# Moving a turned attention tile across partitions: four wide transfers per round in place of sixteen square ones

## The chip, the cores and the metric

The kernel runs on one core of a Trainium2 chip. The metric is device time in microseconds (us), from the first to the last instruction of one execution with what lies around it. Three executions of the kernel before took 3247.21, 3250.87 and 3253.22 us, so the median is 3250.87 us.

The core has five engines with a queue each: PE (TensorE, matrix products, with its weight loads shown apart as PEld), DVE (VectorE), ACT (ScalarE), POOL (GpSimd) and SP (SyncE, which only issues transfers here). Transfers run on 16 DMA engines that all queues share. In the profile a transfer that SP issues is on queue q1 and one that POOL issues on queue q0.

## The reference, cut to what matters

Four batches of 1024 tokens, 256 wide, go through a block of four residual steps: attention A (16 heads of 64), a feed-forward step, attention B (16 heads of 64 with low-rank projections and a rotary turn of q and k), and the same feed-forward step again. Everything is float32. The two attentions share this core:

```python
scores = jnp.einsum('bhsd,bhtd->bhst', q, k) * scale
attn = jax.nn.softmax(scores, axis=-1)
out = jnp.einsum('bhst,bhtd->bhsd', attn, v)
```

So each attention has 4 x 16 score matrices of 1024 queries by 1024 keys. The feed-forward steps are `gelu(x @ w1 + b1) @ w2 + b2` with 1024 hidden values, and the change does not touch them.

## The kernel before, in words

**Tiling.** Heads go in pairs: 4 batches x 8 pairs = 32 groups per attention. A group has 8 steps of 128 queries, so an attention has 256 steps. Two steps make a round (`HB = 2`), so there are 128 rounds per attention and 256 in all. `attention` (L190) lays out pieces of work by step, and `steps_with` (L339) emits them in a fixed order; every engine then works through its own queue in that order.

**One step** `s` does the following for 128 queries and the two heads `j` of the pair:

- `scores` (L238, matmul L247): per head a tile `sc` of 128 queries (partitions) by 1024 keys in PSUM. There are three such buffers.
- `exponentials` (L253): DVE takes the row maximum (L258), and ACT writes `exp` into the tile `p` (L260). Before the change a key's place in the row is split as (k, c, i) with 16 k, 2 c and 32 i, and head `j` fills the columns `c` of its own half, in runs of 64 values.
- `invert` (L266): the reciprocal of the row sum (DVE) is spread by ACT over a 17th block of `p` (L269), so that it travels with the probabilities.
- `turn` (L274): DVE transposes 32x32 blocks of `p` into the tile `T` (L280). Afterwards keys lie along partitions, but only within blocks: the 32 partitions of group `a` hold the keys of query block `a`, and the four key groups `c` lie one after another along the free axis.

**The move.** The product with `v` wants all keys of a head on 64 partitions, so `T` (one per round, two buffers) is copied to `pT` (two buffers), square by square: square (a, c) goes from the 32 partitions of group `a` to the 32 partitions of group `c`, 32 rows of 1,088 values (136 KB). There are 16 squares per round. `squares` orders them so that consecutive ones come from groups two apart (0 and 2, or 1 and 3) and go to groups two apart.

- `send` (L298, transfer L304) issues them: SP the first ones directly after the second `turn` of the round, POOL the last five (`POOL_DMA = 5`) in the next step.
- In attention A (`kept=0`) all 16 squares are sent: 11 by SP, 5 by POOL. In attention B (`kept=1`) square (0, 0) stays on its partitions and ACT copies it (`keep`, L296); SP sends 10 and POOL 5.

**After the move.** Two rounds later (`LAG = 5` steps) `weigh` (L306, matmul L313) multiplies with `v`, `take` (L319) copies the sums (ACT) and scales them by the 17th block (POOL, L325), and in the step after that `project` (L327, matmuls at L176) adds the output projection to the residual (ACT L335, POOL L337).

**What sets the order around the change.** SP's queue holds, in this order, a round's squares and then, at some steps, weight loads (in attention B: `wuq`, `wuk`, `wuv` at L849 and `wo` at L221 and L223). SP's first square of round `h` waits for the second turn of the round, and for `weigh` and `take` of round `h-2`, which used the same `pT` buffer. The first turn of round `h+2` waits until the squares of round `h` have been read out of the `T` buffer. Each queue also has eight completion semaphores for its transfers; a transfer waits until the one that used its semaphore before has landed. POOL carries, besides its five squares, the additions to the residual, the scaling at L325 and, in attention B, the rotary products (L870 to L872) and their two transfers (`turned`, L865).

Of the kernel before, what the change touches and what calls it, by code (L numbers as in the profile page):

```python
# [9 lines left out]
F32 = mybir.dt.float32  # L10
AF = mybir.ActivationFunctionType
# [4 lines left out]
P = 128  # L16
# [9 lines left out]
SQ = 32  # L26
# [3 lines left out]
LAG = 5  # L30
NK = 2 * NT + 1
SENT = NG * HB * NK * SQ
POOL_DMA = 5
NK2 = S // DH
EPS = 1e-5
EARLY = 0.5
# [12 lines left out]
def hybrid_block_kernel(  # L49
# [137 lines left out]
                    start=(i == 0), stop=(i == len(parts) - 1),  # L187
                )

    def attention(prep_batch, prep_pair, wo, loader, lead, kept):  # L190

        pairs = [(b, pr) for b in range(B) for pr in range(NF)]
        steps = [(g, qs) for g in range(len(pairs)) for qs in range(NT)]
        n = len(steps)
        pieces, first = {}, []
        tiles, wos = {}, {}

        def load_out(g):

            wos[g] = wop.tile([P, HB, D], F32, tag="wo", name="wo")
            rows = wo[ts(pairs[g][1], P), :]  # L220
            loader.dma_start(wos[g][:, 0], rows)  # L221
            for j in range(2):
                loader.dma_start(wos[g][ts(j, DH), 1], rows[ts(1 - j, DH), :])  # L223

        for g, (b, pr) in enumerate(pairs):
            for k, f in prep_batch(b) if pr == 0 else ():
                first.append(f) if g == 0 else pieces.setdefault(NT * g - 4 * NT + k, []).append(f)
            tiles[g], load, work = prep_pair(b, pr)
            if g < 2:
                first.insert(g, load)  # L230
            else:
                pieces.setdefault(NT * g - NT - lead - EARLY, []).append(load)
            pieces.setdefault(NT * g - 1 - EARLY, []).append(lambda g=g: load_out(g))
            for k, f in work:
                first.append(f) if g == 0 else pieces.setdefault(max(NT * g - NT + k, -1 - EARLY), []).append(f)
        sc, probs, total, T, pT, av, oT = {}, {}, {}, {}, {}, {}, {}

        def scores(s):  # L238
            g, qs = steps[s]
            qT, kT = tiles[g]["qT"], tiles[g]["kT"]  # L240
            for j in range(2):
                sc[s, j] = ps_sc.tile([P, S], F32, tag="sc", name="sc")
            for m in range(S // 512):
                for half in range(2):
                    for j in range(2):
                        rows = slice(j * DH, (j + 1) * DH)
                        nc.tensor.matmul(  # L247
                            sc[s, j][ts(half, DH), ts(m, 512)],
                            qT()[rows, ts(2 * qs + half, DH)], kT()[rows, ts(m, 512)],
                            start=True, stop=True,  # L250
                        )

        def exponentials(s, j):  # L253
            if j == 0:
                probs[s] = pp.tile([P, NK, NG, SQ], F32, tag="p", name="p")
                total[s] = small.tile([P, 2], F32, tag="total", name="total")
            nmax = small.tile([P, 1], F32, tag="nmax", name="nmax")
            nc.vector.tensor_reduce(nmax, sc[s, j], AX.X, ALU.max, negate=True)  # L258
            place = j ^ (s % HB)
            nc.scalar.activation(  # L260
                probs[s][:, :NK2, ts(j, 2), :],
                sc.pop((s, j)).rearrange("p (k c i) -> p k c i", c=2, i=SQ), AF.Exp,
                bias=nmax, accum_out=total[s][:, place : place + 1],
            )

        def invert(s):  # L266
            t = total.pop(s)
            nc.vector.reciprocal(t, t)  # L268
            nc.scalar.copy(  # L269
                probs[s][:, NK2].rearrange("p (j c) i -> p j (c i)", j=2),  # L270
                t.unsqueeze(2).to_broadcast([P, 2, DH]),
            )

        def turn(s):  # L274
            h, q = divmod(s, HB)
            if q == 0:
                T[h] = tp.tile([P, SENT], F32, tag="T", name="T").rearrange(
                    "p (c q k i) -> p c q k i", c=NG, q=HB, k=NK
                )
            nc.vector.transpose(  # L280
                T[h][:, :, q, :, :].rearrange("p c k i -> p k c i"), probs.pop(s)
            )

        squares = [
            ((a + 2 * i) % NG, (c + 2 * (i ^ x)) % NG)
            for x in range(2) for a in range(2) for c in range(2) for i in range(2)
        ]


        sent = [ac for ac in squares if ac not in [(a, a) for a in range(kept)]]

        def keep(h):
            for a in range(kept):
                nc.scalar.copy(pT[h][ts(a, SQ), a], T[h][ts(a, SQ), a])  # L296

        def send(h, engine, which):  # L298
            if h not in pT:
                pT[h] = ptp.tile([P, SENT], F32, tag="pT", name="pT").rearrange(  # L300
                    "p (a q k i) -> p a q k i", a=NG, q=HB, k=NK
                )
            for a, c in which:
                engine.dma_start(pT[h][ts(c, SQ), a], T[h][ts(a, SQ), c])  # L304

        def weigh(h):  # L306

            v = tiles[HB * h // NT]["v"]()
            av[h] = [group(P) for q in range(HB)]
            for k in range(NK2):  # L310
                for q in range(HB):
                    for j in range(2):
                        nc.tensor.matmul(  # L313
                            av[h][q][ts(j ^ q, DH)], v[ts(j, DH), k, :],
                            pT[h][ts(j, DH), :, q, k, :],
                            start=(k == 0), stop=(k == NK2 - 1),
                        )

        def take(h):  # L319

            oT[h] = otp.tile([P, HB, P], F32, tag="oT", name="oT")
            for q, sums in enumerate(av.pop(h)):
                nc.scalar.copy(oT[h][:, q], sums)  # L323
            parts = oT[h].rearrange("p q (a i) -> p a q i", i=SQ)
            nc.gpsimd.tensor_mul(parts, parts, pT.pop(h)[:, :, :, NK2, :])  # L325

        def project(h):  # L327
            g, t0 = divmod(HB * h, NT)
            b, pr = pairs[g]
            po = group(HB, D)  # L330
            for t in range(HB):
                paired(po[:, t, :], [(oT[h][:, t], [wos[g][:, t]] * 2)])
            oT.pop(h)
            got = tmp.tile([P, HB, D], F32, tag="tmp", name="got")
            nc.scalar.copy(got, po)  # L335
            xd = xs[b][:, t0 : t0 + HB, :]
            nc.gpsimd.tensor_add(xd, xd, got)  # L337

        def steps_with(others):  # L339
            for k, f in others:  # L340
                pieces.setdefault(k, []).append(f)
            for s in range(-1, n + LAG + 1):
                h, part = divmod(s - LAG, HB)
                ahead = 0 <= s + 1 < n
                if 0 <= s < n:
                    invert(s)
                if ahead:
                    scores(s + 1)
                if part == 1 and 0 <= s // HB - 1 < n // HB:
                    send(s // HB - 1, nc.gpsimd, sent[len(sent) - POOL_DMA :])  # L350
                if part == 1 and 0 <= h < n // HB:
                    project(h)
                if ahead:
                    exponentials(s + 1, 0)
                for f in pieces.get(s - EARLY, ()):
                    f()
                if part == 0 and 0 <= h < n // HB:
                    weigh(h)
                if ahead:
                    exponentials(s + 1, 1)  # L360
                if part == 0 and 0 <= h < n // HB:
                    take(h)
                if 0 <= s < n:
                    turn(s)
                if part == 0 and 0 <= s // HB - 1 < n // HB:
                    keep(s // HB - 1)
                    T.pop(s // HB - 1)
                if part == 0 and 0 <= s < n:
                    send(s // HB, nc.sync, sent[: len(sent) - POOL_DMA])
                for f in pieces.get(s, ()):  # L370
                    f()

        return first, steps_with
# [331 lines left out]
    def layer_a():  # L705
# [69 lines left out]

        later = [(4 + i, lambda i=i: rows.measure(2 + i // TQ, i % TQ)) for i in range(6 * TQ)]
        later += [(4 + 6 * TQ, lambda: rows.finish[2]())]
        first, steps = attention(batch_a, pair_a, wo_a, nc.gpsimd, lead=3, kept=0)
        loads, xn, pair = first[:2], first[2:14], first[14:]

        def measured(qb):
# [15 lines left out]
    def layer_b(rows):  # L797
# [92 lines left out]
            work += [(4 + 2 * qb - EARLY, lambda qb=qb: values(qb)) for qb in range(NQB)]  # L890
            return {name: lambda name=name: made[name] for name in ("qT", "kT", "v")}, load, work

        return attention(batch_b, pair_b, wo_b, nc.sync, lead=5, kept=1)


    n_steps = B * NF * NT
# [72 lines left out]
```

## Time and profile before

The profiled execution took 3250.15 us, and its span in the profile is 3248.4 us.

| | before |
|---|---|
| median of three executions | 3250.87 us |
| profiled execution | 3250.15 us |
| span, mean granted clock | 3248.4 us, 0.996 |
| PE busy | 3164.4 us, 97% |
| DVE busy | 2723.5 us, 84% |
| ACT busy | 2137.9 us, 66% |
| POOL busy | 2002.1 us, 62% |
| exponential L260, mean of one | 1119 ns, 1024 of them |
| maximum L258, mean of one | 1218 ns, 1024 of them |
| turn L280, mean of one | 2436 ns, 512 of them |
| square issued by SP / by POOL | 2688 / 1280, 136 KB each, 4.7 us median to landing |
| copied square L296, mean of one | 1096 ns, 128 of them |
| chain that ended last | PE 69%, SP's queue 12%, DMA 6%, DVE 5%, ACT 4% |

Busy time of an engine says how long it had work in hand, not that it set the pace. The question in each stage is which wait ends last there. For the DMA engines the profile gives packets, bytes and the time that packets took as a share of 16 engines' time. A row of a square is one packet of 4,352 bytes, so the time of a row is that share times 16 times the length of the window, divided by the rows in it.

### The profile page before, as it was taken

What the parts mean: (1) busy time and instruction counts of PE and PEld (TensorE: products, weight loads), DVE (VectorE), ACT (ScalarE), POOL (GpSimd) and SP (SyncE); (2) the same over time, 40 slices, a digit from 0 to 9 for tenths busy, and PEclk for the clock granted to TensorE, in tenths of its full rate; (3) what the DMA queues carried; (4) which work ended last, traced back from release to release, by engine and by line L of the source; (5) the groups of instructions that cost most, each with busy time, mean ns of one, the idle gap of its engine ahead of it and who ended that gap; (6) DMA issues with size and microseconds to landing.
All of it is one profiled execution on the core that took longest, in us unless ns stands there. A gap on an engine that the chain in (4) does not pass through costs nothing.

```text
span 3248.4 us, 128967 instructions
## 1 busy us (share of the span) xinstructions
PE 3164.4 (97%) x53648; PEld 2092.2 (64%) x53648; DVE 2723.5 (84%) x2686; ACT 2137.9 (66%) x4400; POOL 2002.1 (62%) x2782
## 2 busy tenths in 40 slices
PE   8999999999999999999999999999999999999999
PEld 4666666666666666668866566666666666655688
DVE  7988888888888888966569989998999999999554
ACT  5666666666666666655447777777778777777542
POOL 4544545455444545442249889899899889886311
PEclk9999999999999999999999999999999999999999
DMA  8888888888888888850029889988989899988200
GB/s 228 217 224 215 224 224 228 217 219 222 221 217 225 219 231 223 221 150 1 4 74 244 225 228 243 242 237 236 246 243 243 234 240 246 238 235 221 57 20 27
DMA packets 244709, 642.29 MB, mean 198 GB/s; under 512 B 74304, under 2 KB 102976, under 8 KB 244128
## 3 DMA queue, kind: packets, MB, share of 16 engines
q1 hardware_dynamic: 161104, 397.60, 48.0%
q0 software_dynamic: 83024, 236.44, 26.0%
q8 instruction: 426, 6.98, 1.0%
q14 instruction: 155, 1.27, 0.1%
HBM read 43.39 MB, written 4.19 MB: 15 GB/s over the span
## 4 chain that ended last, share of the span: by engine, by line
PE 69%; SPq 12%; DMA 6%; DVE 5%; ACT 4%; issue 3%; POOL 1%; DVEq 0%; ACTq 0%; POOLq 0%
PE sc L247 20%; PE mm L313 19%; PE mm L176 15%; SPq L304 11%; DMA pT<-T 5%; PE pw L495 4%; PE mm L185 4%; PE mm L495 3%; PE mm L615 2%; DVE T L280 2%; DVE nmax L258 1%; ACT p L260 1%; PE ph L604 1%; ACT gT L529 1%; PE mm L162 1%
## 5 line engine op out<-in xcount | busy, mean ns | idle before, releaser
L258 DVE TENSOR_REDUCE nmax<-sc 128x1 f32<-128x1024 f32 x1024 | 1204.5, 1218 | 214.3 <-PE sc L247 211.3
L260 ACT ACTIVATE p<-sc,nmax 128x1024 f32<-128x1024 f32 x1024 | 1145.3, 1119 | 322.3 <-DVE nmax L258 322.2
L280 DVE STREAM_TRANSPOSE T<-p 128x2176 f32<-128x2176 f32 x512 | 1247.3, 2436 | 48.4 <-DMA pT<-T 18.4
L247 PE MATMUL sc<-kT,qT 64*64 64x512 f32 x8192 | 1082.5, 598 | 11.9 <-ACT p L260 10.3
L313 PEld LDWEIGHTS mm<-pT,v 64*64 64x64 f32 x32768 | 949.5, 133 | 140.7 <-issue 98.5
L313 PE MATMUL mm<-pT,v 64*64 64x128 f32 x32768 | 983.0, 269 | 9.6 <-issue 8.5
L304 POOL DMA_DIRECT2D pT<-T x1280 | 629.6, 499 | 125.5 <-PE sc L247 57.7
L325 POOL TENSOR_TENSOR oT<-oT,pT 128x256 f32<-128x256 f32 x256 | 187.0, 730 | 696.3 <-ACT oT L323 623.0
L247 PEld LDWEIGHTS sc<-kT,qT 64*64 64x64 f32 x8192 | 332.8, 133 | 401.6 <-issue 274.5
L337 POOL TENSOR_TENSOR x<-x,got 128x512 f32<-128x512 f32 x256 | 331.0, 1293 | 25.8 <-ACT got L335 22.0
L335 ACT COPY got<-mm 128x512 f32<-128x512 f32 x256 | 150.0, 586 | 281.8 <-PE mm L176 281.8
L176 PE MATMUL mm<-wo,oT 128*64 128x256 f32 x2048 | 279.9, 394 | 24.1 <-POOL oT L325 22.8
L176 PEld LDWEIGHTS mm<-wo,oT 128*64 128x64 f32 x2048 | 124.9, 136 | 273.2 <-POOL oT L325 226.5
L269 ACT COPY p<-total 128x128 f32<-128x128 f32 x512 | 151.9, 297 | 198.6 <-DVE total L268 192.4
L176 PE MATMUL mm<-hT,w 128*64 128x512 f32 x1024 | 243.4, 597 | 0.9 <-ACT hT L165 0.9
L260 ACT ACTIVATION_READ_ACCUMULATOR p<-sc,nmax 128x1 f32 x1024 | 205.2, 200 | 0.0
L185 PEld LDWEIGHTS mm<-w,hT 128*64 128x64 f32 x4096 | 140.9, 138 | 71.3 <-issue 69.4
L871 POOL TENSOR_TENSOR turned<-turned,sin_sb 128x512 f32<-128x512 f32 x128 | 163.8, 1279 | 0.0
L409 POOL TENSOR_TENSOR x<-x,b_sb 128x256 f32<-128x256 f32 x64 | 48.8, 777 | 170.6 <-ACT xn L156 170.6
L296 ACT COPY pT<-T 32x1088 f32<-32x1088 f32 x128 | 140.3, 1096 | 4.9 <-DMA pT<-T 1.1
L185 PE MATMUL mm<-w,hT 128*64 128x64 f32 x4096 | 140.9, 222 | 0.2 <-ACT kT L758 0.2
L176 PEld LDWEIGHTS mm<-hT,w 128*64 128x64 f32 x1024 | 73.3, 138 | 96.8 <-issue 75.0
(145 smaller groups left out, 2928.5 us busy)
## 6 DMA issues: line engine op xcount, KB each, us to landing
pT<-T SPq DMA_DIRECT2D x2688, 136.0 KB, 4.7
pT<-T POOLq DMA_DIRECT2D x1280, 136.0 KB, 4.7
turned<-kT POOLq DMA_DIRECT2D x128, 128.0 KB, 3.4
turned<-qT POOLq DMA_DIRECT2D x128, 128.0 KB, 3.5
w<-in_wqkv_a POOLq DMA_DIRECT2D x96, 128.0 KB, 6.0
wo<-in_wo_a POOLq DMA_DIRECT2D x32, 128.0 KB, 5.4
wo<-in_wo_a POOLq DMA_DIRECT2D x64, 64.0 KB, 5.5
wo<-in_wo_b SPq DMA_DIRECT2D x32, 128.0 KB, 4.0
```

What stands on the lines that cost most here:

```text
L176: nc.tensor.matmul(out[ts(j, DH)], lhsT[:, ts(j, DH)], rhs[j], start=(first and i == 0), stop=(last and i == len(parts) - 1),)
L185: nc.tensor.matmul(out[ts(j, DH)], lhsT, rhs[:, ts(j, DH)], start=(i == 0), stop=(i == len(parts) - 1),)
L247: nc.tensor.matmul(sc[s, j][ts(half, DH), ts(m, 512)], qT()[rows, ts(2 * qs + half, DH)], kT()[rows, ts(m, 512)], start=True, stop=True,)
L258: nc.vector.tensor_reduce(nmax, sc[s, j], AX.X, ALU.max, negate=True)
L260: nc.scalar.activation(probs[s][:, :NK2, ts(j, 2), :], sc.pop((s, j)).rearrange("p (k c i) -> p k c i", c=2, i=SQ), AF.Exp, bias=nmax, acc ...
L280: nc.vector.transpose(T[h][:, :, q, :, :].rearrange("p c k i -> p k c i"), probs.pop(s))
L304: engine.dma_start(pT[h][ts(c, SQ), a], T[h][ts(a, SQ), c])
L313: nc.tensor.matmul(av[h][q][ts(j ^ q, DH)], v[ts(j, DH), k, :], pT[h][ts(j, DH), :, q, k, :], start=(k == 0), stop=(k == NK2 - 1),)
L325: nc.gpsimd.tensor_mul(parts, parts, pT.pop(h)[:, :, :, NK2, :])
L337: nc.gpsimd.tensor_add(xd, xd, got)
L495: nc.tensor.matmul(bank[:, t, : right(k).shape[-1]], left(t, k), right(k), start=(first and t == 0 and k == 0), stop=(k == n_k - 1), skip_ ...
L871: nc.gpsimd.tensor_mul(other, other, sin_sb[:, ts(qb, QB)])
```

## The change

The keys of a head are placed differently in a row of `p`. A block of 64 keys is now split as (i, c) with 16 i and 4 c: key `4*i + c` goes to column `c`, place `i`, and head `j` has the places `16*j` to `16*j + 15` of all four columns. After the turn, the four pieces of one partition of `T` (17,408 bytes one after another) are the rows of four consecutive partitions of `pT`. Partition `i` of group `a` becomes partitions `4*i` to `4*i + 3`, and the key order within a head is the same as before. So one query block `a` is one transfer from 32 partitions to all 128 partitions, 128 rows of 4,352 bytes, 544 KB. A round has four of them, all issued by SP directly after the round's second turn. POOL issues none, and ACT's copy `keep` is gone from attention B.

The exponential now reads `sc` in steps of four values and writes runs of 16 values; the spread of the reciprocal at L269 is laid out the same way.

```diff
-POOL_DMA = 5
@@ exponentials
+            half = slice(j * SQ // 2, (j + 1) * SQ // 2)
             nc.scalar.activation(
-                probs[s][:, :NK2, ts(j, 2), :],
-                sc.pop((s, j)).rearrange("p (k c i) -> p k c i", c=2, i=SQ), AF.Exp,
+                probs[s][:, :NK2, :, half],
+                sc.pop((s, j)).rearrange("p (k i c) -> p k c i", c=NG, i=SQ // 2), AF.Exp,
                 bias=nmax, accum_out=total[s][:, place : place + 1],
             )
@@ invert
             nc.scalar.copy(
-                probs[s][:, NK2].rearrange("p (j c) i -> p j (c i)", j=2),
-                t.unsqueeze(2).to_broadcast([P, 2, DH]),
+                probs[s][:, NK2].rearrange("p c (j i) -> p j c i", j=2),
+                t.unsqueeze(2).unsqueeze(3).to_broadcast([P, 2, NG, SQ // 2]),
             )
@@ squares, keep and send
-        squares = [
-            ((a + 2 * i) % NG, (c + 2 * (i ^ x)) % NG)
-            for x in range(2) for a in range(2) for c in range(2) for i in range(2)
-        ]
-        sent = [ac for ac in squares if ac not in [(a, a) for a in range(kept)]]
-        def keep(h):
-            for a in range(kept):
-                nc.scalar.copy(pT[h][ts(a, SQ), a], T[h][ts(a, SQ), a])
-        def send(h, engine, which):
-            if h not in pT:
-                pT[h] = ptp.tile([P, SENT], F32, tag="pT", name="pT").rearrange(
-                    "p (a q k i) -> p a q k i", a=NG, q=HB, k=NK
+        def send(h):
+            pT[h] = ptp.tile([P, SENT], F32, tag="pT", name="pT").rearrange(
+                "p (a q k i) -> p a q k i", a=NG, q=HB, k=NK
+            )
+            for a in range(NG):
+                nc.sync.dma_start(
+                    pT[h][:, a].rearrange("p q k i -> p (q k i)"),
+                    T[h][ts(a, SQ)].rearrange("p c q k i -> p (c q k i)"),
                 )
-            for a, c in which:
-                engine.dma_start(pT[h][ts(c, SQ), a], T[h][ts(a, SQ), c])
@@ steps_with
-                if part == 1 and 0 <= s // HB - 1 < n // HB:
-                    send(s // HB - 1, nc.gpsimd, sent[len(sent) - POOL_DMA :])
@@
-                if part == 0 and 0 <= s // HB - 1 < n // HB:
-                    keep(s // HB - 1)
-                    T.pop(s // HB - 1)
                 if part == 0 and 0 <= s < n:
-                    send(s // HB, nc.sync, sent[: len(sent) - POOL_DMA])
+                    send(s // HB)
+                    T.pop(s // HB)
```

More of the change, by code (lines that the diff above doesn't have):

```diff
@@ L188, in by_head, with attention @@
                 )
-    def attention(prep_batch, prep_pair, wo, loader, lead, kept):
+    def attention(prep_batch, prep_pair, wo, loader, lead):
         pairs = [(b, pr) for b in range(B) for pr in range(NF)]
@@ L777, in layer_a @@
         later += [(4 + 6 * TQ, lambda: rows.finish[2]())]
-        first, steps = attention(batch_a, pair_a, wo_a, nc.gpsimd, lead=3, kept=0)
+        first, steps = attention(batch_a, pair_a, wo_a, nc.gpsimd, lead=3)
         loads, xn, pair = first[:2], first[2:14], first[14:]
@@ L891, in pair_b @@
             return {name: lambda name=name: made[name] for name in ("qT", "kT", "v")}, load, work
-        return attention(batch_b, pair_b, wo_b, nc.sync, lead=5, kept=1)
+        return attention(batch_b, pair_b, wo_b, nc.sync, lead=5)
     n_steps = B * NF * NT
```

## The prediction

> **What bounds the kernel now.** I read the page's busy times first, then busy time by stage, the DMA queues of the same stages, and last single microseconds of the DMA record. Busy time by stage, attention A and then attention B (columns: stretch, length, busy PE, PEld, DVE, ACT, POOL with instruction counts, granted clock, DMA share, GB/s):
>
> ```profile
> 200.00:1400.00 1200.00, 1197.89 (x22991) 757.50 (x22985) 1054.40 (x898) 777.86 (x1688) 594.76 (x929) 1.00 0.86 222
> 1800.00:2950.00 1150.00, 1122.58 (x20869) 710.97 (x20872) 1051.07 (x903) 883.35 (x1770) 1029.38 (x1336) 1.00 0.90 238
> ```
>
> PE has 2 us free in A and 27 us in B, so PE sets the pace of both. Directly behind it stand the DMA engines, 86% and 90% busy. Their queues, A first:
>
> ```profile
> q1 hardware_dynamic: 58204, 168.97, 56.3%
> q0 software_dynamic: 33271, 94.16, 28.8%
> ...
> pT<-T SPq DMA_DIRECT2D x1211, 136.0 KB, 4.7
> pT<-T POOLq DMA_DIRECT2D x550, 136.0 KB, 4.4
> ```
>
> ```profile
> q1 hardware_dynamic: 72698, 165.66, 56.1%
> q0 software_dynamic: 36884, 105.25, 32.2%
> ...
> pT<-T SPq DMA_DIRECT2D x1098, 136.0 KB, 4.8
> pT<-T POOLq DMA_DIRECT2D x548, 136.0 KB, 5.1
> ```
>
> SP sends 11 squares a round in A and 10 in B, so 1211/11 = 110.1 rounds in 1200 us are 10.90 us a round, and 1098/10 = 109.8 in 1150 us are 10.47 us. A row of a square is one packet of 4,352 bytes. On q1 in A, where nothing else runs, a row took 0.563 x 16 x 1200 us / (1211 x 32) = 279 ns, with several squares in flight from both queues. What a row takes when only one square is in flight shows after a pause of the queues. Three such moments (0.9, 0.7 and 0.7 us long):
>
> ```profile
> DMA packets 32, 0.14 MB, mean 155 GB/s; under 512 B 0, under 2 KB 0, under 8 KB 32
> q1 hardware_dynamic: 32, 0.14, 72.0%
> ```
>
> ```profile
> DMA packets 33, 0.14 MB, mean 199 GB/s; under 512 B 1, under 2 KB 1, under 8 KB 33
> q1 hardware_dynamic: 33, 0.14, 91.5%
> ```
>
> ```profile
> q1 hardware_dynamic: 33, 0.14, 90.1%
> ```
>
> The 32 rows of the lone square took 0.720 x 16 x 0.9 us / 32 = 324 ns each, then 0.915 x 16 x 0.7 / 32 = 320 and 315 ns. So a square alone is slower per row than squares among others (279 ns), though nothing competes with it. The competition must be inside the square: its 16 engines all read the same 32 partitions and write the same 32. Against that, the start-up load of `x`, 128 partitions wide and 1,024 bytes a packet, over 4.5 us:
>
> ```profile
> DMA packets 1392, 1.47 MB, mean 328 GB/s; under 512 B 48, under 2 KB 1360, under 8 KB 1392
> q1 hardware_dynamic: 1344, 1.34, 88.8%
> ```
>
> That is 0.888 x 16 x 4.5 us / 1344 = 48 ns per 1,024 bytes, or 202 ns per 4,352 bytes. I infer that the spread over partitions sets the pace, and that `squares`, which alternates groups two apart, lets two squares in flight use different ways into the memory.
>
> **The change part by part.**
>
> *The four wide transfers.* Bytes in A stay: 4 x 128 rows are the 512 rows of 16 squares, 32 per DMA engine and round. In B the copied square returns: 30 rows per engine become 32. The destination is now 128 partitions, but every transfer reads 32 partitions, and the four stand one behind another in one queue, so all engines read the same group together. That is the lone square's reading side without its writing side. The bounds for a row are 202 ns (the wide load, if only the destination counts) and 648 ns (twice the lone square, if engines are dealt to rows in a way that crowds the reading more). The nearest row is the lone square in attention A, and I take 324 ns.
>
> The rest of a round's DMA time, from the fences by bytes: a square is 0.1393 MB. In A the squares are all of q1 and 76.6 of q0's 94.16 MB; the other 17.6 MB are 5.4% of 10.90 us, 0.59 us. In B the squares are 152.9 of 165.66 MB on q1 and 76.3 of 105.25 on q0, which leaves 4.3% + 8.8% of 10.47 us, 1.37 us. Instruction fetches on the two remaining queues add 1.2 to 1.3%, 0.13 and 0.14 us. So the DMA engines need
>
> - A: 32 x 0.324 + 0.72 = 11.09 us a round, against 10.90 now: +0.19 us x 128 = 24 us;
> - B: 32 x 0.324 + 1.51 = 11.88 us a round, against 10.47 now: +1.41 us x 128 = 180 us.
>
> The path of the end then runs through DMA: the first turn of round `h+2` waits for round `h`'s transfers to leave the `T` buffer, and `weigh` waits for their landing. The engines can be kept fed meanwhile: after the release DVE needs two turns and two maxima, 2 x 2.44 + 2 x 1.22 = 7.3 us, less than the 11 us that the other round's transfers run. At 279 ns a row the needs are 9.65 and 10.44 us, under today's rounds, and nothing would be lost; the loss starts at (10.90 - 0.72)/32 = 318 ns in A and (10.47 - 1.51)/32 = 280 ns in B.
>
> [...]
>
> *POOL's five issues.* 1280 x 499 ns = 630 us leave POOL, 2.5 us a round. POOL has 595 of 1200 us busy in A (issues counted), and PE is full there, so nothing comes of it. In B POOL is 1029 of 1150 us busy, and it is PE's largest direct wait there: the projection (L176) waited 18.2 us for POOL's scaling (L325). The gain is between 0 and PE's free 27 us; with DMA the bound I take 0.
>
> *SP.* Eleven or ten issues of 596 ns become four. If an issue of 128 rows costs as much, 2.4 us; if it costs by rows, four times that, 9.5 us, still within a round and ahead of the rows. The first issue waits as before for the turn and for `weigh` and `take` of round `h-2`. Queued behind it are the weight loads of B (L221, L849), needed steps later. I take 0.
>
> *ACT.* The copy L296 goes: 128 x 1096 ns = 140 us off ACT in B, which stands 267 of 1150 us idle; 0. The exponential (1119 ns) keeps its 1024 values but reads in steps of four and writes runs of 16. No ACT row here reads in steps. It cannot gain, as it is one pass over the same values; upwards the farthest ACT row is the short copy L269, 297 ns for 128 values, or 2376 ns at 1024 (about a factor of two). Nearest is the exponential itself, so I take 1119. L269 writes its 128 values in shorter runs: between 297 ns and, by the same factor of two, 0.6 us, which is 0.6 us more a round, inside ACT's free 3.8 us in A; 0.
>
> *Sum.* The profiled execution took 3250.15 us (span 3248.4), 0.7 us under the median. 3250 + 24 + 180 = 3454; I predict 3455 us.
>
> **The rivals.**
>
> 1. *The exponential gets slower by its steps.* ACT is free (1200 - 777.9)/110.1 = 3.83 us a round in A, 0.96 us for each of four exponentials; in B 2.43 us and the copy's 1.10, 0.88 us each. Above that ACT is the bound. At the far end, +1.26 us each, ACT needs 7.07 + 5.03 = 12.1 us in A and 8.05 - 1.10 + 5.03 = 12.0 in B: 128 x (1.2 + 1.5) = 346 us, or 3596. Its queue also holds the `oT` copies between exponential and projection; a wait of 0.6 us there per round gives 3750. For it: nothing here reads in steps. Against: the scattered output of the turn costs DVE nothing visible (2436 ns for 2176 values, 1.12 ns each, against 1.19 for the maximum).
>
> [...]
>
> 2. *Crowding is worse.* At 648 ns a row the rounds are 21.5 and 22.2 us: 128 x (10.6 + 11.8) = 2867, or 6117 us. For it: how rows are dealt to engines when 32 partitions feed 128 is not visible. Against: the lone square, the only 32-partition reading seen, shows half of that.
>
> 3. *Faster.* If rows run below 280 ns, because engines drift apart or because the wide destination is what counts, DMA is no bound, and POOL's 2.5 us a round takes away late scaling in B. That wins at most PE's 27 us there and some us at the ramps; 3225 us.
>
> 4. *Nothing comes of it:* rows between 279 and 285 ns, POOL's relief hidden behind a full PE; 3250 us.
>
> **How the numbers follow.** Chances: the forecast 0.45, rival 1 0.22, rival 2 0.10, rival 3 0.16, rival 4 0.07. The forecast's own range runs from 3290 (rows of 290 ns: A hidden, B 0.32 us x 128 = 41) to 3625 (345 ns: 110 + 266 us). The range of 8 in 10 leaves out rival 2 and the upper end of rival 1: 3215 to 3760. A difference under 0.2% cannot be told from none with this kernel. Faster is rival 3, 0.16; same is rival 4, 0.07; slower is the rest, 0.77.
>
> **What would show it.** DMA share near 1 in both stages; rows of 4,352 bytes at 320 to 330 ns on q1; PE waiting at `weigh` (L313) and DVE at the turn for `pT<-T`; rounds of 11.1 and 11.9 us; POOL lighter by 2.5 us a round. Wrong would be: L260 far above 1119 ns (rival 1), rows near 650 (rival 2), or rows under 280 and PE full (rivals 3 and 4).

## The result, and the profile after

Four executions of the changed kernel took 3723.52 to 3764.34 us, with a median of 3736.12 us; four of the kernel before, beside them, have a median of 3249.65 us. The ratio is 1.150, interval 1.144 to 1.156: the change costs 15%, or some 486 us. The profiled execution took 3732.73 us and its span is 3731.0 us, 482.6 us more than the span of before.

Busy time by stage of the kernel after, with the columns of the answer for before (the stretches are again in the middle of attention A and of attention B):

```profile
200.00:1400.00 1200.00, 1139.87 (x20894) 709.73 (x20888) 956.65 (x806) 710.97 (x1546) 295.83 (x351) 0.99 0.94 203
2150.00:3350.00 1200.00, 1027.47 (x16991) 596.22 (x16987) 846.92 (x718) 633.05 (x1351) 622.53 (x645) 0.96 0.92 197
```

PE has lost its full line: 60 us free in A and 173 us in B, and its granted clock in B went down to 0.96. The DMA engines are 94% and 92% busy and move fewer GB/s than before (203 and 197, against 222 and 238). They work longer for nearly the same bytes (659 MB in the whole run, 642 before). POOL is lighter, as it should be (296 of 1200 us busy in A, 595 before). The DMA queue of SP in the same stretches, A first:

```profile
q1 hardware_dynamic: 57785, 223.55, 88.9%
...
pT<-T SPq DMA_DIRECT2D x403, 544.0 KB, 9.6
```

```profile
q1 hardware_dynamic: 68261, 210.62, 85.3%
...
pT<-T SPq DMA_DIRECT2D x360, 544.0 KB, 10.3
```

403/4 = 100.75 rounds in 1200 us are 11.91 us a round in A, and 360/4 = 90 are 13.33 us in B; before they were 10.90 and 10.47. A row in A took 0.889 x 16 x 1200 us / (403 x 128) = 331 ns. In B the transfers are 200.5 of q1's 210.62 MB, so by bytes 81.2 of the 85.3%, which gives 338 ns. A transfer lands 9.6 to 10.3 us after its issue, about twice as late as a square.

The page of the kernel after: the chain that ended last, by engine and by line, then the groups of the turn, the exponential, the product with `v` and the rotary product:

```profile
PE 36%; DMA 21%; SPq 19%; issue 9%; DVE 8%; ACT 4%; POOL 2%; DVEq 0%; POOLq 0%; ACTq 0%
...
L280 DVE STREAM_TRANSPOSE T<-p 128x2176 f32<-128x2176 f32 x512 | 1248.5, 2439 | 555.0 <-DMA pT<-T 448.6
...
L260 ACT ACTIVATE p<-sc,nmax 128x1024 f32<-128x1024 f32 x1024 | 1143.8, 1117 | 258.9 <-DVE nmax L257 258.9
...
L305 PE MATMUL mm<-pT,v 64*64 64x128 f32 x32768 | 1008.6, 276 | 182.9 <-DMA pT<-T 90.9
...
L858 POOL TENSOR_TENSOR kT<-kT,cos_sb 128x512 f32<-128x512 f32 x64 | 81.6, 1275 | 229.7 <-DMA turned<-kT 229.7
L858 POOL TENSOR_TENSOR qT<-qT,cos_sb 128x512 f32<-128x512 f32 x64 | 81.7, 1276 | 227.5 <-DMA turned<-qT 227.5
```

Before, the chain was 69% PE. Now DMA and SP's queue hold 40% of it. DVE stands idle 555 us ahead of the turn, 448.6 us of it for the `T` buffer to be read out. PE waits 91 us for `pT` itself. The exponential takes 1117 ns, as long as before. POOL waits 457 us for the rotary transfers, which land after 6.4 and 6.1 us (before: 3.4 and 3.5; in the kernel with short rows below: 3.2 and 3.4).

The wait for the `T` buffer closes a loop with SP's issues. This is the chain in the middle of B, in order of time (start and length in us):

```profile
2498.24 3.00 SPq L293
2501.28 3.13 SPq L293
2504.46 2.06 SPq L293
2506.57 10.82 DMA pT<-T
...
2520.00 2.25 DVE nmax L257 x2
2522.25 1.31 DVE T L280
...
2524.74 2.92 SPq L293
```

Three issues by SP take 8.3 us, the fourth transfer lands 10.8 us after its issue began, and DVE's turns and maxima with short waits take 7.3 us until SP can issue again. That is 26.5 us for two rounds, since there are two `T` buffers: 13.25 us a round. Over all of B (2150 to 3350 us) SP's issues of `pT` are 31% of the chain and its landings 28%, and SP waited for another engine in only 55 of the 1200 us. In A (200 to 1400 us) the matrix products still have 58% of the chain, the landings 15% and SP's issues 8%.

One moment tells where the longer rows come from. After a pause of the queue, a wide transfer of the kernel after starts alone:

```profile
DMA packets 40, 0.17 MB, mean 116 GB/s; under 512 B 0, under 2 KB 0, under 8 KB 40
q1 hardware_dynamic: 40, 0.17, 102.0%
```

The window is 1.5 us long, so its 40 rows took 1.020 x 16 x 1.5 us / 40 = 612 ns each, nearly twice the 320 ns of a lone square. (A packet counts wholly in the window it starts in, so the share can pass 100%.) The mean of 331 ns is a mixture, which the single packet records of the trace show: in A 53% of the rows took 200 ns or less, and 27% took 450 ns or more. That the long rows come while the engines stand together, and the short ones when they have drifted apart, is my reading; the records name no engine.

### The profile page after: what moved, and what is told of

It reads as the page before. It is cut to its first block, busy times and chain, and to the rows that moved or that the text cites. A ratio compares the mean times of both kernels' runs of the same rounds, so it can differ in the third digit from the quotient of the medians.

```text
span 3731.0 us, 121529 instructions
## 1 busy us (share of the span) xinstructions
PE 3375.2 (90%) x53648; PEld 2141.2 (57%) x53648; DVE 2712.7 (73%) x2686; ACT 2012.3 (54%) x4272; POOL 1370.2 (37%) x1502
## 4 chain that ended last, share of the span: by engine, by line
PE 36%; DMA 21%; SPq 19%; issue 9%; DVE 8%; ACT 4%; POOL 2%; DVEq 0%; POOLq 0%; ACTq 0%
DMA pT<-T 19%; SPq L293 17%; PE mm L305 9%; PE sc L246 9%; PE mm L175 7%; PE pw L483 4%; DVE nmax L257 3%; PE mm L483 3%; DVE T L280 3%; PE mm L184 2%; ACT p L260 2%; PE mm L603 2%; POOL oT L317 1%; DMA turned<-kT 1%; SPq L837 1%
## 5 line engine op out<-in xcount | busy, mean ns | idle before, releaser
L280 DVE STREAM_TRANSPOSE T<-p 128x2176 f32<-128x2176 f32 x512 | 1248.5, 2439 | 555.0 <-DMA pT<-T 448.6
L260 ACT ACTIVATE p<-sc,nmax 128x1024 f32<-128x1024 f32 x1024 | 1143.8, 1117 | 258.9 <-DVE nmax L257 258.9
L246 PE MATMUL sc<-kT,qT 64*64 64x512 f32 x8192 | 1201.9, 610 | 77.2 <-issue 39.8
L305 PE MATMUL mm<-pT,v 64*64 64x128 f32 x32768 | 1008.6, 276 | 182.9 <-DMA pT<-T 90.9
L305 PEld LDWEIGHTS mm<-pT,v 64*64 64x64 f32 x32768 | 960.9, 137 | 345.0 <-issue 280.6
L246 PEld LDWEIGHTS sc<-kT,qT 64*64 64x64 f32 x8192 | 349.5, 134 | 572.2 <-issue 351.6
L269 ACT COPY p<-total 128x128 f32<-128x128 f32 x512 | 152.5, 298 | 718.1 <-DVE total L268 716.6
L175 PE MATMUL mm<-wo,oT 128*64 128x256 f32 x2048 | 287.9, 400 | 54.8 <-POOL oT L317 47.9
L858 POOL TENSOR_TENSOR kT<-kT,cos_sb 128x512 f32<-128x512 f32 x64 | 81.6, 1275 | 229.7 <-DMA turned<-kT 229.7
L858 POOL TENSOR_TENSOR qT<-qT,cos_sb 128x512 f32<-128x512 f32 x64 | 81.7, 1276 | 227.5 <-DMA turned<-qT 227.5
L175 PE MATMUL mm<-hc,w 128*64 128x512 f32 x512 | 138.6, 608 | 0.8 <-issue 0.8
L315 ACT COPY oT<-mm 128x128 f32<-128x128 f32 x512 | 109.8, 267 | 53.8 <-PE mm L305 53.4
```

The source lines that it names most:

```text
L175: nc.tensor.matmul(out[ts(j, DH)], lhsT[:, ts(j, DH)], rhs[j], start=(first and i == 0), stop=(last and i == len(parts) - 1),)
L246: nc.tensor.matmul(sc[s, j][ts(half, DH), ts(m, 512)], qT()[rows, ts(2 * qs + half, DH)], kT()[rows, ts(m, 512)], start=True, stop=True,)
L260: nc.scalar.activation(probs[s][:, :NK2, :, half], sc.pop((s, j)).rearrange("p (k i c) -> p k c i", c=NG, i=SQ // 2), AF.Exp, bias=nmax, a ...
L280: nc.vector.transpose(T[h][:, :, q, :, :].rearrange("p c k i -> p k c i"), probs.pop(s))
L305: nc.tensor.matmul(av[h][q][ts(j ^ q, DH)], v[ts(j, DH), k, :], pT[h][ts(j, DH), :, q, k, :], start=(k == 0), stop=(k == NK2 - 1),)
```

## The experiments

Two theories stood against each other at the start. **S**, the source: 16 DMA engines that start together read neighbouring partitions, and rows read side by side slow each other (a lone square's 320 ns a row, against 279 among others, was the sign). The prediction and the expectations picture this as ways into or out of the memory that neighbours share; that is a guess, and no trace shows such ways. **D**, the shape: few source partitions feeding many destinations, one large transfer, or one queue for everything is what costs. The row times below are all made like those above, from q1's share in 200 to 1400 us (A), and the lone rows from the start of a transfer after a pause.

### Another order of the same four transfers

```diff
-            for a in range(NG):
+            for a in (0, 2, 1, 3):
```

> The changed kernel, with its four transfers issued in the order 0, 2, 1, 3 instead of 0, 1, 2, 3; all still from SP. Theory S (source crowding: all engines read the same 32 partitions at a time, and rows of 4,352 bytes take about 330 ns whatever the destination): each engine still works through one transfer's eight rows before it comes to the next, so two transfers overlap only at their seams; rows 310 to 335 ns, time 3640 to 3740 us. Rival Q (one queue: SP alone feeds the engines, and the loss is from POOL's second queue being gone): the same time as the changed kernel, 3700 to 3760 us. Rival L (landing: transfers of 544 KB land 10 us after issue, and the turn waits for that with two buffers of T): the same, 3700 to 3760 us.

Measured: 3544.31 us, ratio 1.088 (1.086 to 1.091). Consecutive transfers now come from groups two apart, as consecutive squares did. That gives back 192 of the 486 us, more than S had expected and where the rivals Q and L had expected nothing, and a row in A falls from 331 to 302 ns. A lone transfer starts as slowly as before (622 ns a row). So which source partitions are read together matters a good deal, at equal sizes, counts and queue. It does not explain all: DMA is now only 88% busy in both attentions, with rounds of 11.62 and 12.08 us.

### The same transfers over two queues

```diff
-            for a in range(NG):
-                nc.sync.dma_start(
+            for a in (0, 2, 1, 3):
+                (nc.sync if a < 2 else nc.gpsimd).dma_start(
```

> The changed kernel, with transfers 0 and 1 issued by SP and 2 and 3 by POOL at the same point of the order, so that groups two apart are read at the same time from two queues. Theory S: rows fall to 250 to 280 ns, DMA needs 9 to 10.5 us a round, and the time returns to 3230 to 3300 us. Rival Q expects 3230 to 3300 us as well, since two queues feed the engines again. Rival L: a transfer still carries 544 KB and shares the engines with another one, so it lands no earlier; 3500 us or more.

Measured: 5034.78 us, ratio 1.547 (1.543 to 1.550). The expectation failed by a wait that it had not named. The page of this kernel, chain by line, one group and the landing times:

```profile
DMA turned<-qT 18%; DMA turned<-kT 17%; PE sc L246 10%; PE mm L305 10%; PE mm L175 8%; POOL turned L859 3%; POOL pT L293 3%; PE pw L483 3%; PE mm L184 2%; PE mm L483 2%; DMA pT<-T 2%; POOL oT L317 2%; POOL qT L858 2%; POOL kT L858 1%; POOL turned L853 1%
...
L858 POOL TENSOR_TENSOR qT<-qT,cos_sb 128x512 f32<-128x512 f32 x64 | 81.0, 1266 | 802.0 <-DMA turned<-qT 802.0
...
turned<-qT POOLq DMA_DIRECT2D x128, 128.0 KB, 14.9
```

The rotary transfers of attention B stand on POOL's queue behind the 544 KB transfers and land after 14.9 us; POOL waits 802 + 761 us for them, and PE waits 1018 us for POOL's scaling. The rows did not fall to the 250 to 280 ns that S had expected: in A they took 397 ns on SP's queue, 0.439 x 16 x 1200 us / (166 x 128), and by bytes 248 ns on POOL's. With the DMA engines only 76% busy in A and 58% in B (2400 to 4700 us), this run does not settle what two queues cost or save.

### Squares from one queue, in two orders

The kernel before, with all squares issued by SP, and then also in order of the source:

```diff
-POOL_DMA = 5
+POOL_DMA = 0
```

> The kernel before with all squares issued by SP (POOL issues none): 16 a round in attention A, 15 in B, in the order that alternates groups two apart. Theory S: rows stay at 265 to 290 ns; 16 issues of 0.6 us are 9.6 us a round, inside the round, so 3240 to 3330 us. Rival Q: rows of 320 ns and more and 3500 to 3750 us. Rival L: squares land in about 5 us, so 3240 to 3330 us.

```diff
-        squares = [
-            ((a + 2 * i) % NG, (c + 2 * (i ^ x)) % NG)
-            for x in range(2) for a in range(2) for c in range(2) for i in range(2)
-        ]
+        squares = [(a, c) for a in range(NG) for c in range(NG)]
```

> The same as the run with all squares on SP, but the squares in order of their source group: all four of group 0, then of 1, 2 and 3. Theory S: now the engines read one group for four squares in a row, as in the changed kernel; rows 315 to 340 ns and 3550 to 3750 us. Rival Q: the same as that run. Rival L: the same as that run, 3240 to 3330 us, as each square is as small as before.

Measured: 3537.59 us (1.086, 1.0835 to 1.0885) and 3525.91 us (1.083, 1.080 to 1.085). The chain of the first one, by engine and by line:

```profile
SPq 58%; PE 15%; issue 9%; DMA 7%; DVE 5%; ACT 4%; POOL 3%; DVEq 0%; ACTq 0%; POOLq 0%
SPq L304 56%; DMA pT<-T 6%; PE pw L495 4%; PE mm L495 3%; PE mm L176 3%; DVE nmax L258 2%; PE mm L615 2%; POOL x L337 2%; PE sc L247 1%; PE mm L313 1%; DVE T L280 1%; POOL oT L325 1%; ACT p L260 1%; ACT gT L529 1%; ACT got L335 1%
```

SP alone does not keep up. An issue takes 0.59 us (median), but 1627 squares in the 1200 us of A are one in 0.74 us, 11.8 us a round. Its issues are 56% of the chain, and a square lands 2.9 us after its issue, sooner than the 4.7 us of the kernel before, so the DMA engines are not late. S's expected times failed for that reason. The rows took 288 ns in A, and 290 ns in order of the source, where S had expected 315 to 340; with squares issued this slowly the second run can't tell what the order of sources costs. What the pair shows is that POOL's five issues are worth 270 to 280 us to the kernel before.

### The source two and four partitions apart

Nothing but the source partitions of the four transfers changes; for these runs the values that land are others than the reference wants.

```diff
-                    T[h][ts(a, SQ)].rearrange("p c q k i -> p (c q k i)"),
+                    T[h][a::NG].rearrange("p c q k i -> p (c q k i)"),
```

> The changed kernel, with each wide transfer reading every fourth of all 128 partitions (32 rows, four apart) instead of 32 neighbouring ones. Number, size, order, queue and destination of the transfers stay; it moves other values, so what is computed is not the reference. Theory F (reading in fours: several engines that start together read neighbouring partitions that share one way out, as the lone wide transfer's 612 to 666 ns a row suggests, four times 166 ns): the 32 rows no longer share, rows of 4,352 bytes at 170 to 220 ns, DMA share under 0.75, PE full again and 3200 to 3250 us. Rival D (the destination, the size of 544 KB or SP as the only queue is the cause): nothing changes, rows at 330 ns and 3690 to 3770 us.

```diff
-                    T[h][ts(a, SQ)].rearrange("p c q k i -> p (c q k i)"),
+                    T[h][a // 2 * DH + a % 2 : (a // 2 + 1) * DH : 2].rearrange("p c q k i -> p (c q k i)"),
```

> The same with every second partition of a half of 64 (32 rows, two apart), again with other values than the reference's. Theory F: two engines share one way out instead of four, so a lone transfer's rows are near 330 ns, rows on average 220 to 290 ns, and the time lies between the two others, 3230 to 3400 us. Rival D: 3690 to 3770 us. A rival that only counts how many of the 128 partitions' halves a transfer reads (64 partitions of one half are no better than 32) expects 3690 to 3770 us too.

Measured: with the step of four 3233.79 us, ratio 0.992 (0.9905 to 0.9935); with the step of two 3493.34 us, 1.073 (1.070 to 1.076). Busy time in attention A, DMA queue and chain of the kernel with the step of four:

```profile
200.00:1400.00 1200.00, 1197.07 (x22930) 756.72 (x22929) 1051.00 (x898) 775.49 (x1686) 321.76 (x380) 1.00 0.59 221
```

```profile
q1 hardware_dynamic: 63360, 245.13, 53.7%
...
pT<-T SPq DMA_DIRECT2D x441, 544.0 KB, 5.2
```

```profile
PE 84%; ACT 4%; DVE 3%; DMA 3%; issue 3%; SPq 2%; POOL 2%; POOLq 0%; ACTq 0%; DVEq 0%
```

A row took 0.537 x 16 x 1200 us / (441 x 128) = 183 ns, DMA fell from 94% to 59% busy, and PE is full again. A transfer that starts alone, over 0.5 us:

```profile
q1 hardware_dynamic: 38, 0.17, 91.5%
```

That is 0.915 x 16 x 0.5 / 38 = 193 ns, against 612. With the step of two a lone row took 329 ns as expected, but one in A took 308 ns, not 220 to 290, and the time lies above the 3230 to 3400 us that were expected. The size of the transfer, the number of rows, the 32 source and 128 destination partitions, the single queue and SP are the same in all three. D falls: which source partitions are read makes the whole loss. In this pair the step and the range that the 32 partitions span grow together; the runs below part them. This also gives the rest of the change its price. With the DMA engines out of the way it wins 26.6 us against its own runs of before (3260.34).

### Half as wide, from 32 neighbouring partitions

The kernel before with two neighbouring squares in one transfer: 32 partitions to 64, 272 KB, eight per round, all from SP, and no copied square.

```diff
+        parts_of = ((0, 0), (2, 1), (1, 0), (3, 1), (0, 1), (2, 0), (1, 1), (3, 0))
+            for a, j in parts_of:
+                nc.sync.dma_start(
+                    pT[h][ts(j, DH), a].rearrange("p q k i -> p (q k i)"),
+                    T[h][ts(a, SQ), ts(j, 2)].rearrange("p c q k i -> p (c q k i)"),
+                )
```

(The exponential's view is split as (k, i, c) with two `c`, to match.)

> A kernel between the two: a head's 32 + 32 keys of a block are spread in twos, so a round has eight transfers from 32 partitions to 64 (272 KB each), all from SP, one after another from groups two apart; no copied square, nothing issued by POOL; the exponential reads in steps of two. It computes the reference. Theory F: with two source rows for each engine's share, two engines read neighbouring partitions at a time as in a lone square (320 ns), and transfers from groups two apart mix to 260 to 290 ns; eight issues of 0.6 us leave SP free; 3220 to 3290 us. If it is dealt to the engines like the wide transfer, in fours, rows are 330 ns and more and 3400 to 3700 us. Rival D (size and one queue): 3400 us or more as well, with the landing time near 10 us.

Measured: 3461.0 us, 1.061 (1.060 to 1.063). A lone transfer takes 662 ns a row over 1.2 us, and the mean in A is 297 ns. So it starts like the wide transfer and not like a square, and the time is not the 3220 to 3290 us that F had expected. My guess of how rows are dealt to the engines (two source rows each, in order) would have put it near the square.

### The deciding pair: 16 partitions, two apart or next to each other

Theory S, with its groups of four neighbours, fits the lone rows so far: 612 ns from neighbours, 329 two apart, 193 four apart. The four is an estimate from these. Both kernels split each wide transfer in two of 272 KB, in the same order, all from SP. The one takes the even and the odd partitions of a group, the other its first and its second half:

```diff
-            half = slice(j * SQ // 2, (j + 1) * SQ // 2)
+            half = slice(j, SQ, 2)
...
+            for a, j in ((0, 0), (2, 1), (1, 0), (3, 1), (0, 1), (2, 0), (1, 1), (3, 0)):
+                nc.sync.dma_start(
+                    pT[h][ts(j, DH), a].rearrange("p q k i -> p (q k i)"),
+                    T[h][a * SQ + j : (a + 1) * SQ : 2].rearrange("p c q k i -> p (c q k i)"),
+                )
```

> This kernel computes the reference: each wide transfer becomes two of 272 KB, each from 16 partitions two apart (the even or the odd ones of a group of 32) to 64 partitions, eight per round, all from SP, alternating between groups two apart. Theory S (what costs is that the engines start together on neighbouring partitions, and four neighbours share one way out): 16 engines on 16 partitions two apart use eight ways, so a lone transfer runs at about 330 ns a row as a lone square does, the mean in both attentions falls to 260 to 300 ns, and the time is 3230 to 3350 us. Rival U (what costs is that few partitions feed many, whichever they are): 16 partitions are fewer still than 32, so rows stay at 330 ns or more in the mean and the time is 3500 to 3800 us. The exponential writes every second place; by the step-of-four reading that cost nothing I expect 1119 ns.

```diff
-                    T[h][a * SQ + j : (a + 1) * SQ : 2].rearrange("p c q k i -> p (c q k i)"),
+                    T[h][ts(2 * a + j, SQ // 2)].rearrange("p c q k i -> p (c q k i)"),
```

> The same eight transfers of 272 KB in the same order, but each from 16 neighbouring partitions (the first or the second half of a group of 32). It computes the reference. Theory S: 16 engines on 16 neighbours use four ways, so a lone transfer runs at about 650 ns a row, the mean stays above 300 ns in both attentions, and the time is 3500 to 3700 us, at least 5% over the kernel with the step of two. Rival U: the same time as with the step of two, within 1%.

Measured: two apart 3338.25 us, 1.025 (1.023 to 1.027); neighbours 3871.72 us, 1.189 (1.186 to 1.192). The lone starts, two apart (0.8 us) and neighbours (1.3 us):

```profile
DMA packets 33, 0.14 MB, mean 180 GB/s; under 512 B 0, under 2 KB 0, under 8 KB 33
q1 hardware_dynamic: 33, 0.14, 84.4%
```

```profile
DMA packets 35, 0.15 MB, mean 117 GB/s; under 512 B 0, under 2 KB 0, under 8 KB 35
q1 hardware_dynamic: 35, 0.15, 102.3%
```

0.844 x 16 x 0.8 / 33 = 327 ns and 1.023 x 16 x 1.3 / 35 = 608 ns, as S expected (330 and 650). The times fall at 3338 inside the range expected, and at 3872 above it. The rival U of these expectations falls too: 16 partitions are not slow because they are few. Nor does the range count for a lone start: 16 neighbours take 608 ns and 32 neighbours 612, 16 two apart take 327 ns (within the same 32 partitions) and 32 two apart, over 64, take 329. In A 21% of the single rows take 450 ns or more with neighbours, and 2% two apart. In the kernel with neighbours SP's issues became 49% of the chain (median 1444 ns each, against 752), so part of its time comes by way of that queue.

Busy time by stage of the kernel with the step of two:

```profile
200.00:1400.00 1200.00, 1184.71 (x22624) 749.48 (x22620) 1035.06 (x883) 781.62 (x1660) 317.37 (x375) 1.00 0.90 218
1900.00:2900.00 1000.00, 942.68 (x17257) 611.39 (x17248) 862.53 (x726) 667.97 (x1373) 633.13 (x655) 0.99 0.99 239
```

Here A is nearly whole (PE 1185 of 1200 us), and in B the DMA engines are the bound at 99%: what is left of the loss is the forecast's mechanism at smaller rows (289 ns in A, 0.833 x 16 x 1200 us / (866 x 64)). Of the kernels with wider transfers that leave the computation whole this is the fastest, and it is still 2.5% behind the kernel before. Its exponential, which writes every second place, took 1214 ns and not the 1119 expected.

### What the size of a transfer costs, and POOL once more

The 544 KB transfers with the step of two (other values than the reference's, as above) in the order 0, 2, 1, 3:

```diff
-            for a in range(NG):
+            for a in (0, 2, 1, 3):
```

> The four 544 KB transfers with a step of two in the source (two groups of 64 partitions, even and odd; other values are moved than the reference wants, as in the earlier run with that step), now issued in the order 0, 2, 1, 3, so that consecutive ones read different halves. Theory S adds that alternating halves lets two transfers in flight use different ways: rows fall from about 300 to about 285 ns, as with the 272 KB transfers that alternate. If the size of a transfer costs nothing of its own, the time is that of those, 3310 to 3370 us. If a 544 KB transfer also leaves DMA engines without work at its end, which the 272 KB ones do not, the rows fall likewise, but the DMA share stays at 0.90 to 0.95 in both attentions and the time is 3400 to 3470 us.

Measured: 3422.29 us, 1.052 (1.050 to 1.054), the second of the two branches. Busy time by stage:

```profile
200.00:1400.00 1200.00, 1162.45 (x21948) 735.52 (x21940) 1005.70 (x853) 743.03 (x1614) 309.37 (x366) 1.00 0.89 213
1900.00:2900.00 1000.00, 906.22 (x16514) 567.78 (x16510) 835.91 (x702) 619.64 (x1325) 606.18 (x629) 0.99 0.94 229
```

In B the DMA engines are 94% busy where the 272 KB transfers of the step of two filled them to 99%. So some of the time in which DMA engines stand idle goes with the larger transfer (and with its smaller count and its wider destination, which these runs don't separate). How is not shown: 25% of the chain there are the landings of the rotary transfers, against 5% with the 272 KB transfers. The step alone does not set how busy the DMA engines are. In this order neighbours have 88% in both attentions, against 89% and 94% here; in the order 0, 1, 2, 3 neighbours have 94% and 92%, against 90% and 93% two apart.

The 272 KB transfers with the step of two, the last two of a round from POOL in the next step, where the kernel before has its five squares:

```diff
+                if part == 1 and 0 <= s // HB - 1 < n // HB:
+                    send(s // HB - 1, nc.gpsimd, sent[6:])
...
-                    send(s // HB)
+                    send(s // HB, nc.sync, sent[:6])
```

> The 272 KB transfers from 16 partitions two apart, six of them from SP and the last two from POOL, at the place where the kernel before issues its five squares from POOL (it computes the reference). Theory S: two queues have transfers from different groups in flight at once, so the mean row falls from 286 towards the 265 ns of the kernel before, and the time is 3240 to 3300 us: no better than the kernel before by more than 0.5%, since PE is full there. If instead POOL's queue makes its own two transfers and the rotary ones behind them late, as with half of the transfers on POOL, attention B gets slower and the time is 3400 us or more.

Measured: 3512.21 us, 1.080 (1.077 to 1.083), slower by 174 us than with SP alone, so the time that S expected failed. The row's price did not fall (about 300 ns on SP's queue), and `pT` lands after 7.8 and 7.3 us in place of 6.3. The other branch named the rotary transfers, but those land after 4.8 and 4.5 us, no later than with SP alone (4.6 and 4.7). What makes it slower is not settled: PE's waits before the product with `v` grew (127 us, against 18), but the profile names no releaser for them.

## Why the prediction was right or wrong

The direction was right, and the time fell into the range. The predicted loss, 204 us, was less than half of the measured one.

**What held.** The DMA engines became nearly full (94% and 92%) and PE lost its full line, the turn waits for the `T` buffer to be read out, and `weigh` waits for `pT`. POOL's issues went, and no gain from it shows in the changed kernel. With short rows the rest of the change is worth 26.6 us, where rival 3 had allowed 27 in B and some at the ramps. The exponential kept its 1119 ns: 1117. With that rival 1 falls: the read in steps of four cost nothing. L269 measured 298 ns, as predicted.

**The step that failed: "The engines can be kept fed meanwhile", with SP's issues at 0.** The prediction made the round equal to the DMA engines' work. That work came out close to its terms: 0.94 x 11.91 = 11.20 us in A (predicted 11.09) and 0.92 x 13.33 = 12.27 us in B (11.88). But the rounds last 11.91 and 13.33 us. In 128 rounds each:

| | A | B |
|---|---|---|
| forecast | 24 us | 180 us |
| more DMA work than predicted | 0.11 x 128 = 14 | 0.39 x 128 = 50 |
| DMA engines without work | 0.71 x 128 = 91 | 1.06 x 128 = 136 |

Together 495 us, against 482.6 us between the spans. So 227 of the missing 291 us are time in which some DMA engines had nothing to do while the round still waited for transfers. I had compared DVE's 7.3 us with 11 us of transfers and left out SP's issues ("still within a round and ahead of the rows"). In the chain they stand on the path: 8.3 us of issues, 10.8 us to the last landing and DVE's 7.3 us make the 26.5 us of two rounds in B, 13.25 us a round against 12.27 us of DMA work. An issue took 2424 ns (median), so four took 9.7 us, near my upper bound of 9.5 us; with short rows (the step of four, 183 ns) it took 616 ns, so I read the slow rows as what held SP back. In B SP was on the path already before the change: from 1800 to 2950 us its issues are 25% of the chain, where I had read from PE's busy time that PE sets the pace.

Why single DMA engines run out of work is not shown. The packet records of A have fewer than 16 packets in flight for 50% of the time, and 8 or fewer for 1.4%, so half of the time at least one engine has nothing in flight, and seldom do most of them. Engines that read at uneven rates would do that, but no run parts this from SP's slow issues.

**The row's size was nearly right by luck, for a wrong reason.** 324 ns were taken from the lone square, 331 and 338 measured as means. But the lone wide transfer does not run at the lone square's rate: it takes 612 ns, as rival 2's crowding (648 ns) has it. Rival 2's mistake was the other half: that the crowding lasts. Only part of the rows stay that long (27% took 450 ns or more in A), and the mean falls to half of it.

**The inference "the spread over partitions sets the pace" held, sharper than I put it.** Among the transfers that feed 64 or 128 partitions, a lone row's time goes by the step between the source partitions (608 to 662 ns from neighbours, 327 and 329 with a step of two, 193 with a step of four), and neither by their number (16 neighbours 608, 32 neighbours 612) nor by their range (two apart within 32 partitions 327, over 64 partitions 329). That it is the spread of the 16 partitions read at one moment fits this. But the lone square reads 32 neighbours too and takes 320 ns, so the step alone does not explain it. How rows are dealt to the engines may count as well, and that is not seen.

**Rival 3's mechanism is real, but its condition was not met here:** rows under 280 ns and a full PE are what the step of four shows (183 ns, 1197 of 1200 us in A), at 3234 us against its predicted 3225. I found no layout that has it with this turn, where 32 neighbouring partitions hold one query block.

## What to carry to other kernels

Before making transfers larger, look at which partitions the DMA engines read at the same moment: a transfer that starts alone shows it in one microsecond of the DMA record (here 612 ns a row against 193). The step of four was worth 502 us to the changed kernel and the order that alternates distant groups 192 us, while four transfers in place of sixteen, with all else that changed, won 26.6 us once the rows were short. And when a forecast makes DMA the bound, don't set the round equal to the DMA work: follow the loop through the buffer, with the issues and the last landing in it. At 92 and 94% busy, the unfilled part was 227 us, nearly half of the loss.

## What was unexpected in the hardware

- Lone transfers at the same 4,352 bytes a row: 612 ns from 32 neighbours to 128 partitions, 329 ns with a step of two, 193 ns with a step of four. Which engine takes which row is not seen; the transfer from 32 to 64 partitions (662 ns) did not fit my guess.
- An issue by SP took 616 ns (median) where a row took 183 ns and 2424 ns where it took 331 ns, for the same 544 KB.
- The exponential reads in steps of four at no cost (1117 ns, 1119 before) but takes 1214 ns where it writes every second place of a row in place of runs of 16.
